# Moving a softmax scaling from VectorE to ScalarE, and choosing anew which sums of x live in DRAM, in a two-layer graph attention kernel

## The chip, the core and the metric

The kernel runs on one core of one Trainium2 chip. The metric is the time of one execution on the device in microseconds (us): the median over runs. The profiled execution's own time is given beside it, because all durations come from that one execution.

## What is computed

A two-layer graph attention network over 512 nodes with 768 features, 16,896 edges (one self-loop per node among them), eight heads of 768 features in the first layer and one in the second, then a residual and a layer norm:

```python
def gat_layer(x, W, a_s, a_d, b, edge_index, concat):
    h = (x @ W).reshape(n, H, C)
    alpha_s = jnp.einsum('nhc,hc->nh', h, a_s)
    alpha_d = jnp.einsum('nhc,hc->nh', h, a_d)
    e = jax.nn.leaky_relu(alpha_s[src] + alpha_d[dst], NEG_SLOPE)
    m = jax.ops.segment_max(e, dst, num_segments=n)
    e = jnp.exp(e - m[dst])
    denom = jax.ops.segment_sum(e, dst, num_segments=n)
    alpha = e / (denom[dst] + EPS)
    out = jax.ops.segment_sum(h[src] * alpha[:, :, None], dst, num_segments=n)
    return out.reshape(n, H * C) + b

h = gat_layer(x, W1, a_src1, a_dst1, b1, edge_index, concat=True)
h = jax.nn.elu(h)
out = gat_layer(h, W2, a_src2, a_dst2, b2, edge_index, concat=True)
return _layernorm(x + out, axis=-1)
```

All of it is in float32.

## The kernel before

**The attention matrix.** Because there are only 512 nodes, the kernel counts the edges into a dense 512 x 512 matrix once (`cnt`), and each head's attention is then a dense softmax. A softmax tile `q` is 128 target nodes by 512 source nodes, so a head has four tiles. For one tile: `lift` (L572, ScalarE) adds the two logits, `leak` (L576, VectorE) is the leaky ReLU, `rank` (L581 VectorE, L583 ScalarE) takes the row maximum and the exponential, and `weigh` (L788 to L798, VectorE) multiplies by the counts with a running row sum (L791), makes the reciprocal `rden` (L794, L795) and scales the tile by it (L797). Then `turn_out` transposes it: ScalarE splits the 32-bit values into 16-bit halves (L812, into `pS` for tiles 0 to 2 and into `nr` for tile 3), and a transposing DMA goes out on SP's queue (L814); later `turn_in` puts the halves together again on ScalarE (L817) into `PT`, the transposed attention matrix.

**The stages of a head.** The loop over heads h = 0 to 6 handles, in this order, three matrix products that belong to three heads:

1. `mixed(h)` (L867, matmuls at L889), the aggregation: features of head h times its attention matrix, as seven products of halves (Strassen's scheme) for each of three column blocks; ELU on ScalarE (L826 to L828), result into `gT` (L829, VectorE). Work of VectorE for other stages is handed in as the list `fill` and dealt out between its steps by `some`.
2. `second(h)` (L442, matmuls at L364): the result times this head's rows of W2, added up in `h2` and `u2` (VectorE, L459). Again seven products, P1, P2, P6, P7, P4, P5, P3, each for two row blocks (`pairs`). P3 goes into the bank that P5 was emptied from. Between these products the softmax of head h + 1 is written: for n = 2 to 6 the loop issues the pair n of products, one tile's `leak` and `rank`, a `weigh` and `turn_out`, and the emptyings `e0` and `e1`. All of `attend` (L985) and of the list `in_second` also goes between them.
3. For head h + 2 the projection x @ W1. For heads 3 to 7 it is `by_thirds` (L407, matmuls at L423; "the thirds stage" below): a scheme of 15 products of blocks of thirds, each product one step of eight matmul records, in the order P8, P13, P9, P2, P4, P12, P6, P0, P1, P10, P5, P14, P11, P7, P3. Five PSUM banks (a, x, b, y, z) take turns: a bank must be emptied (L429 on ScalarE, L431 on VectorE) before the next step may use it. Head 2 has `projection` (L382, matmuls at L364), fourteen products.

Instruction order on each engine is the program's order; nothing is moved by a scheduler.

**The sums of x.** The thirds scheme needs nine sums of blocks of x. They are made once, by VectorE, around head 1 (`x_thirds`, L922): P8, P9 and P13 in place of blocks of `xT`; four in `xF`, the storage of `xS`, which is free after head 2's projection; and five in `gF`, the storage of `gT`. But `gT` is overwritten by every head's aggregation. So the five are stored once to DRAM (`store`, L940, from L936 to L938's results) and loaded again in each round h = 1 to 5 (`reload_x`, L948, `gT<-xd`, 1280 KB) once the second product of head h no longer reads `gT`. The reload stands on SP's queue behind the four transposing DMAs of the softmax and the load of a block of W1 (L161). The five were P7, P1, P6, P3, P14; of these P6 is the first that the thirds stage reads, at its seventh step. The sums are dealt over the stages around head 1: `early` (and `again_`, which restores a block of `xT` that the previous scheme had changed) in head 2's projection, `late_[0]` at its thirteenth product, the next two behind the aggregation of head 1, and four in the second product of head 1.

Of the kernel before, what the change touches and what calls it, by code (L numbers as in the profile page):

```python
# [13 lines left out]
AF = mybir.ActivationFunctionType  # L14
# [22 lines left out]
def gat_pass(  # L37
# [16 lines left out]
    nc = tc.nc  # L54
# [9 lines left out]
    HK = DC // 2  # L64
    HN = N // 2
# [63 lines left out]
    def square(t_, j):  # L129
        return t_[:, j * 2 * TH:(j + 1) * 2 * TH].rearrange("p (k n) -> p k n", k=2)  # L130
# [116 lines left out]
    for j in range(2):  # L247
        nc.vector.tensor_reduce(picks[:, j:j + 1], ident.rearrange("p (j k) -> p k j", k=32)[:, j, :], axis=AX.X,
                                op=ALU.add)
# [5 lines left out]
    xT = keep.tile([P, DC, N], F32, name="xT")  # L255
# [121 lines left out]
    def logits(h, feats, t):  # L377
        for al, a, sign in zip(AL[h], A[h], (1.0, -1.0)):
            nc.vector.scalar_tensor_tensor(scr, feats[:, t, :], sign, a, op0=ALU.mult,  # L379
                                           op1=ALU.mult, accum_out=al[:, t:t + 1])  # L380
# [219 lines left out]
    if not general:  # L600
# [95 lines left out]
        for n, batch in enumerate(batches):  # L696
# [32 lines left out]
            if n + 1 == len(batches):  # L729
                spread(0)  # L730
                q = [lift(0, t) for t in range(NT)]
# [11 lines left out]
    else:  # L743
# [26 lines left out]
        q = [lift(0, t) for t in range(NT)]  # L770
# [17 lines left out]
    def weigh(q, t, scale=True):  # L788

        den = small.tile([P, 1], F32, name="den")  # L790
        nc.vector.scalar_tensor_tensor(q, q, 1.0, cnt[:, t, :], op0=ALU.mult, op1=ALU.mult,  # L791
                                       accum_out=den)
        rden = small.tile([P, 1], F32, name="rden")
        nc.vector.tensor_scalar(rden, den, EPS_DEN, None, op0=ALU.add)  # L794
        nc.vector.reciprocal(rden, rden)  # L795
        if scale:
            nc.vector.tensor_scalar(q, q, rden, None, op0=ALU.mult)  # L797
        return rden  # L798
# [7 lines left out]

    parted = {}

    def turn_out(q, t):
        apart = pS[:, t].rearrange("p k n -> p (k n)") if t < 3 else work.tile([P, N], F32, name="nr")  # L810
        apart = apart.bitcast(U16)
        nc.scalar.copy(apart.rearrange("p (h n) -> p h n", h=2), q.bitcast(U16).rearrange("p (n h) -> p h n", h=2))  # L812
        parted[t] = work.tile([P, N], F32, name="zr", bufs=3).bitcast(U16)
        nc.sync.dma_start(parted[t].rearrange("p (j d) -> p j d", d=P), apart, transpose=True)  # L814
# [103 lines left out]
    gF, xF = gT.rearrange("p c n -> p (c n)"), xS.rearrange("p a k n -> p (a k n)")  # L918
# [3 lines left out]
    def x_thirds():  # L922

        a = {(i, k): xT[:, 2 * k:2 * k + 2, i * TH:(i + 1) * TH] for i in range(2) for k in range(3)}
        X = dict(P2=a[0, 0], P4=a[1, 2], P0=a[1, 1], P8=a[0, 2], P13=a[0, 1], P9=a[1, 0])
        X.update({p: square(gF, j) for j, p in enumerate(("P7", "P1", "P6", "P3", "P14"))})
        X.update({p: square(xF, j) for j, p in enumerate(("P11", "P10", "P12", "P5"))})

        def op(o, u, v, how):
            return lambda: nc.vector.tensor_tensor(o, u, v, op=how)  # L930

        def negative(o, u, v):
            return lambda: nc.vector.scalar_tensor_tensor(o, u, -1.0, v, op0=ALU.mult, op1=ALU.subtract)

        plus, minus = ALU.add, ALU.subtract
        early = [op(X["P7"], a[0, 0], a[0, 1], minus), op(X["P1"], X["P7"], a[0, 2], minus),  # L936
                 op(X["P6"], a[1, 2], X["P1"], minus), op(X["P3"], a[0, 2], a[0, 0], minus),
                 negative(X["P14"], a[0, 2], a[1, 2])]  # L938
        again_ = op(xT[:, :HK, HN:], xT[:, :HK, :HN], xT[:, :HK, HN:], minus)
        store = lambda: nc.sync.dma_start(stored, gF[:, :RELOAD * 2 * TH])  # L940
        late_ = [op(X["P10"], X["P1"], a[1, 1], minus), op(X["P11"], a[0, 1], a[1, 1], plus),
                 negative(X["P12"], a[0, 0], a[1, 1]), op(X["P8"], a[1, 0], a[1, 2], minus),
                 op(X["P5"], X["P10"], X["P8"], plus), op(X["P9"], a[1, 0], a[1, 1], minus),
                 negative(X["P13"], a[0, 0], a[1, 2])]
        return X, early, again_, store, late_

    def reload_x():
        nc.sync.dma_start(gF[:, :RELOAD * 2 * TH], stored)  # L948
# [38 lines left out]
        return [times(slice(0, D), b2_[:, :D], 1.0, V[:, :, 0]), times(L, b2_[:, D:], -1.0, V[:, :, 1]),  # L987
                times(R, b1_[:, D:], -1.0, V2)]

    behind, in_second = [], []  # L990
    for h in range(H - 1):
        if 0 < h < H - 2:
            B3, rest_of_thirds = load_thirds(h + 2)
# [11 lines left out]
        besides, behind = [], []  # L1005
# [25 lines left out]
        q = [lift(h + 1, 0)]  # L1031
        for n in range(2, 7):
            (m0, e0), (m1, e1) = pairs[2 * n:2 * n + 2]
            m0()
            if not last:
                m1()
            if n < 6:
                leak(q[n - 2])
                rank(q[n - 2], n - 2)
            if n < 5:  # L1040
                q.append(lift(h + 1, n - 1))
            if last:

                if n > 4:
                    turn_in(n - 5)
                if n == 6:
                    turn(q[2], 2)
                if n == 6:
                    weigh(q[3], 3)
                m1(lambda: turn(q[3], 3) if n == 6 else None)  # L1050
            if not last and n == 6:
                turn_in(0)
                weigh(q[2], 2)
                turn_out(q[2], 2)
            e0()
            if last and 2 < n < 6:
                weigh(q[n - 3], n - 3)
                if n < 5:
                    turn_out(q[n - 3], n - 3)
            if not last and 3 < n < 6:  # L1060
                weigh(q[n - 4], n - 4)
                turn_out(q[n - 4], n - 4)
            if not last and n == 6:
                weigh(q[3], 3)
                turn_out(q[3], 3)
                if 0 < h:
                    sums = rest_of_thirds()
                    reload_x()
                load_w2(h + 1)()
            e1()  # L1070
            for f in in_second[:1]:
                f()
            del in_second[:1]
            if 0 < h and not last and 2 < n < 6:
                attend[n - 3]()
        if 0 < h and h + 2 < H:
            pairs = by_thirds(h + 2, XB, B3)
            AA, sums3 = left_sums(h + 1)
            B2, sums2 = right(W2[h + 1], "w1")
            for n in range(15):  # L1080
                pairs[n][0]()
                for p in {0: ("P6", "P2"), 1: ("P4",), 4: ("P10",), 5: ("P0",), 6: ("P1",), 9: ("P7",),
                          12: ("P3",)}.get(n, ()):
                    sums[p]()
                if n == 5:
                    BB, rsums_ = right_sums()
                    sums3 += rsums_
                if n in (2, 3, 5, 6, 8, 9, 10):
                    for _ in range(2 if n == 8 else 1):
                        sums3.pop(0)()  # L1090
                if n in (11, 13):
                    logits(h + 2, HS[h + 2], 2 + (n - 11) // 2)
                if n == 14:
                    sums2[0]()
                    behind = sums2[1:]
                pairs[n][1]()
                if n in (1, 2, 4):
                    turn_in((n + 2) // 2)
            assert not sums3
        elif h + 2 < H:  # L1100
            B_, sums = right(W1[h + 2], "w2")
            pairs = projection(h + 2, XA, B_)
            for n in range(14):
                pairs[n][0]()
                if n == 0:
                    for f in attend:
                        f()
                    B2, sums2 = right(W2[h + 1], "w1")
                if n in (1, 3):
                    sums[n // 2]()  # L1110
                if n == 1:
                    AA, sums3 = left_sums(h + 1)
                pairs[n][1]()
                if n in (1, 2, 4):
                    turn_in((n + 2) // 2)
                if n == 5:
                    BB, sums3 = right_sums()
                if 1 <= n < 9:
                    sums3.pop(0)()
                if n == 0:  # L1120
                    XB, early, again_, store, late_ = x_thirds()
                if n in (2, 4, 6, 8, 9):
                    early.pop(0)()
                if n == 9:
                    store()
                if n == 9:
                    again_()
                if n == 12:
                    late_.pop(0)()
                    sums2.pop(0)()  # L1130
                    behind = sums2 + late_[:2]
                    in_second = late_[2:]
                if n in (11, 13):
                    logits(h + 2, HS[h + 2], 2 + (n - 11) // 2)
        else:
            last_sum()
            B2, sums2 = right(W2[H - 1], "w1")
# [162 lines left out]
```

## Time and profile before

| What | Value |
|---|---|
| median of 3 runs | 648.23 us (647.3 to 649.41) |
| the profiled execution | 647.71 us, its span 645.9 us |
| TensorE matmul busy | 630.7 us, 98% |
| TensorE weight loads busy | 434.9 us, 67% |
| VectorE busy | 535.4 us, 83% |
| ScalarE busy | 289.8 us, 45% |
| GpSimd busy | 63.6 us, 10% |
| DMA moved | 109.87 MB, mean 170 GB/s |
| granted TensorE clock | 0.999 |

Columns of a timeline row: start and length in us, engine, line, operation, output <- inputs, how many were merged, and in brackets the idle time just ahead and what ended it. PE is TensorE, PEld its weight loads, DVE VectorE, ACT ScalarE, POOL GpSimd, SP the engine that issues most DMAs; SPq is its instruction queue. A group's row has line, engine, operation, names, shapes and count, then busy us and mean ns of one, then the idle time ahead. In a list of waits: us in total, times, longest. A matmul of float32 stands in the trace as more than one record.

### The profile page before, as it was taken

What the parts mean: (1) busy time and instruction counts of PE and PEld (TensorE: products, weight loads), DVE (VectorE), ACT (ScalarE), POOL (GpSimd) and SP (SyncE); (2) the same over time, 40 slices, a digit from 0 to 9 for tenths busy, and PEclk for the clock granted to TensorE, in tenths of its full rate; (3) what the DMA queues carried; (4) which work ended last, traced back from release to release, by engine and by line L of the source; (5) the groups of instructions that cost most, each with busy time, mean ns of one, the idle gap of its engine ahead of it and who ended that gap; (6) DMA issues with size and microseconds to landing.
All of it is one profiled execution on the core that took longest, in us unless ns stands there. A gap on an engine that the chain in (4) does not pass through costs nothing.

```text
span 645.9 us, 7667 instructions
## 1 busy us (share of the span) xinstructions
PE 630.7 (98%) x2509; PEld 434.9 (67%) x2509; DVE 535.4 (83%) x1162; ACT 289.8 (45%) x486; POOL 63.6 (10%) x105
## 2 busy tenths in 40 slices
PE   8999999999999999999999999999999999999995
PEld 5555586556756786588857886588857886544553
DVE  8989889988889778878789778878789778876775
ACT  5875655520726045441726145441726145543440
POOL 1210011010200220010200220010200210000000
PEclk9999999999999999999999999999999999999999
DMA  8994488796905976198815986198924991310122
GB/s 300 324 219 97 103 219 289 154 268 223 238 9 112 315 209 183 21 271 222 230 76 115 308 225 172 20 259 230 231 79 108 326 294 33 95 59 1 28 63 77
DMA packets 86845, 109.87 MB, mean 170 GB/s; under 512 B 40151, under 2 KB 67983, under 8 KB 86031
## 3 DMA queue, kind: packets, MB, share of 16 engines
q1 hardware_dynamic: 70590, 87.42, 41.9%
q0 software_dynamic: 15776, 21.30, 19.8%
q10 hardware_dynamic: 432, 0.59, 0.3%
q8 instruction: 22, 0.36, 0.2%
q14 instruction: 25, 0.20, 0.1%
HBM read 95.12 MB, written 2.90 MB: 152 GB/s over the span
## 4 chain that ended last, share of the span: by engine, by line
PE 88%; DMA 5%; DVE 4%; ACT 1%; issue 1%; DVEq 0%; SPq 0%; ACTq 0%
PE mm L364 41%; PE mm L889 19%; PE mm L423 15%; DMA gT<-xd 5%; PE mm L835 3%; PE mm L1246 3%; PE held L364 2%; PE tr L664 1%; PE bc L233 1%; PE held L544 1%; PE bc L664 0%; DVE h L459 0%; ACT os L636 0%; DVE scr L379 0%; PE mm L262 0%
## 5 line engine op out<-in xcount | busy, mean ns | idle before, releaser
L364 PE MATMUL mm<-w,gT 128*128 128x384 f32 x252 | 83.6, 486 | 0.0
L364 PEld LDWEIGHTS mm<-w,gT 128*128 128x128 f32 x252 | 47.9, 190 | 31.9
L583 ACT ACTIVATE q<-q,nmax 128x512 f32<-128x512 f32 x36 | 25.8, 721 | 96.3 <-DVE nmax L581 96.3
L889 PE MATMUL mm<-PT,hs 128*128 128x256 f32 x252 | 61.3, 379 | 0.0
L364 PE MATMUL mm<-w1t,gS 128*128 128x384 f32 x180 | 60.6, 487 | 0.0
L429 ACT ACTIVATE hs<-mm 128x512 f32<-128x512 f32 x30 | 17.9, 596 | 91.6 <-PE mm L423 91.2
L889 PEld LDWEIGHTS mm<-PT,hs 128*128 128x128 f32 x252 | 47.8, 190 | 7.3 <-issue 0.4
L364 PEld LDWEIGHTS mm<-w1t,gS 128*128 128x128 f32 x180 | 34.1, 190 | 24.0 <-DVE w1t L356 0.5
L459 DVE TENSOR_TENSOR h<-h,mm 128x384 f32<-128x384 f32 x72 | 39.0, 549 | 11.8 <-PE mm L364 11.5
L431 DVE TENSOR_TENSOR hs<-hs,mm 128x512 f32<-128x512 f32 x45 | 30.8, 684 | 21.3 <-PE mm L423 21.3
L889 PE MATMUL mm<-pS,gS 128*128 128x256 f32 x168 | 43.2, 380 | 0.0
L817 ACT COPY PT<-zr 128x1024 uint16<-128x1024 uint16 x34 | 39.3, 1155 | 2.6 <-DMA zr<-pS 1.9
L423 PE MATMUL mm<-w2r,xT 128*128 128x256 f32 x160 | 37.8, 379 | 0.0
L423 PE MATMUL mm<-w2r,gT 128*128 128x256 f32 x160 | 37.5, 382 | 0.0
L812 ACT COPY pS<-q 128x1024 uint16<-128x1024 uint16 x26 | 27.1, 1044 | 18.3 <-DVE q L797 18.3
L889 PEld LDWEIGHTS mm<-pS,gS 128*128 128x128 f32 x168 | 31.8, 190 | 4.7 <-DVE pS L862 0.4
L423 PEld LDWEIGHTS mm<-w2r,xT 128*128 128x128 f32 x160 | 30.4, 190 | 5.2
L423 PEld LDWEIGHTS mm<-w2r,gT 128*128 128x128 f32 x160 | 30.0, 190 | 5.8 <-DVE hs L431 1.9
L364 PE MATMUL mm<-w1t,gT 128*128 128x384 f32 x96 | 32.3, 486 | 0.0
L364 PE MATMUL mm<-w,gS 128*128 128x384 f32 x84 | 29.3, 495 | 1.1 <-DVE h L459 1.1
L638 DVE TENSOR_SCALAR os<-nodes,idx 128x512 bf16<-128x512 f16 x104 | 29.0, 352 | 1.4 <-PE tr L664 1.4
L893 ACT COPY u<-mm 128x256 f32<-128x256 f32 x21 | 7.8, 372 | 49.2 <-PE mm L889 49.2
(233 smaller groups left out, 1260.5 us busy)
## 6 DMA issues: line engine op xcount, KB each, us to landing
w2r<-in_L_gnn_W_dram SPq DMA_DIRECT2D x48, 384.0 KB, 11.0
w<-in_L_gnn_W_dram SPq DMA_DIRECT2D x43, 384.0 KB, 10.9
gT<-xd SPq DMA_DIRECT2D x5, 1280.0 KB
w1t<-in_L_gnn_W_dram SPq DMA_DIRECT2D x9, 576.0 KB
w<-in_L_gnn_W_dram POOLq DMA_DIRECT2D x8, 576.0 KB, 8.5
w1t<-in_L_gnn_W_dram POOLq DMA_DIRECT2D x7, 576.0 KB, 9.6
w2t<-in_L_gnn_W_dram SPq DMA_DIRECT2D x15, 256.0 KB, 7.1
w2t<-in_L_gnn_W_dram POOLq DMA_DIRECT2D x15, 256.0 KB, 8.8
```

The lines of the kernel that those rows point to most:

```text
L364: nc.tensor.matmul(ps[:, :HALF], A_[p][:, k, i * P:(i + 1) * P], B_[p][:, k, :], start=start and k == 0, stop=k == HK - 1, skip_group_chec ...
L423: nc.tensor.matmul(bank[chain][:, i * TH:(i + 1) * TH], A_[p][:, k, i * P:(i + 1) * P], B_[p][:, k, :], start=first and i == k == 0, stop= ...
L429: nc.scalar.activation(out(o), ps, AF.Copy, scale=how)
L431: nc.vector.tensor_tensor(out(o), out(o), ps, op=how)
L459: nc.vector.tensor_tensor(a, a, ps, op=ALU.subtract if p == "P7" else ALU.add)
L583: nc.scalar.activation(q, q, AF.Exp, bias=nmax, scale=-1.0)
L638: nc.vector.tensor_scalar(o, nodes, idx[:, c:c + 1], None, op0=ALU.is_equal)
L812: nc.scalar.copy(apart.rearrange("p (h n) -> p h n", h=2), q.bitcast(U16).rearrange("p (n h) -> p h n", h=2))
L817: nc.scalar.copy(PT.rearrange("p s n -> p (s n)").bitcast(U16).rearrange("p (s n h) -> p s n h", s=NT, h=2)[:, :, t * P:(t + 1) * P, :], p ...
L835: nc.tensor.matmul(ps[:, :N], HS[h][:, s, c * P:(c + 1) * P], PT[:, s, :], start=(s == 0), stop=(s == NT - 1))
L889: nc.tensor.matmul(bank[p][:, :HN], A_[p][:, k, c * P:(c + 1) * P], B_[p][:, k, :], start=over is None and k == 0, stop=k == 1, skip_group ...
L1246: nc.tensor.matmul(ps[:, :cols.stop - cols.start], PT[:, s, t * P:(t + 1) * P], h2[:, s, cols], start=(s == 2), stop=(s == 1))
```

## The change

There are two edits.

The scaling of a softmax tile by `rden` moves for heads 1 to 6: `weigh` is called with `scale=False` and returns `rden`, and `turn_out` begins with an ACTIVATE of ScalarE that copies `q` onto itself times `rden`, ahead of the copy that splits it. Heads 0 and 7 keep VectorE's scaling, the second layer had none.

The sums of x: in `gF`, and so in DRAM, are now P7, P1, P3, P14, P11; in `xF` are P10, P6, P12, P5. The first sum that the thirds stage reads from `gT` is thus P1, at its ninth step. The work is dealt out anew: six operations in `early` (P7, P1, P3, P14, the restoring one, P11), the store behind the last of them, P10 and P6 at the thirteenth and fourteenth product of head 2's projection, P8 in the aggregation of head 1, P13 and P9 in its second product, and P12 and P5 at the third and eighth step of head 3's thirds stage.

```diff
-    def turn_out(q, t):
+    def turn_out(q, t, rden=None):
+        if rden is not None:
+            nc.scalar.activation(q, q, AF.Copy, scale=rden)
...
-        X.update({p: square(gF, j) for j, p in enumerate(("P7", "P1", "P6", "P3", "P14"))})
-        X.update({p: square(xF, j) for j, p in enumerate(("P11", "P10", "P12", "P5"))})
+        X.update({p: square(gF, j) for j, p in enumerate(("P7", "P1", "P3", "P14", "P11"))})
+        X.update({p: square(xF, j) for j, p in enumerate(("P10", "P6", "P12", "P5"))})
...
         early = [op(X["P7"], a[0, 0], a[0, 1], minus), op(X["P1"], X["P7"], a[0, 2], minus),
-                 op(X["P6"], a[1, 2], X["P1"], minus), op(X["P3"], a[0, 2], a[0, 0], minus),
-                 negative(X["P14"], a[0, 2], a[1, 2])]
-        again_ = op(xT[:, :HK, HN:], xT[:, :HK, :HN], xT[:, :HK, HN:], minus)
+                 op(X["P3"], a[0, 2], a[0, 0], minus), negative(X["P14"], a[0, 2], a[1, 2]),
+                 op(xT[:, :HK, HN:], xT[:, :HK, :HN], xT[:, :HK, HN:], minus), op(X["P11"], a[0, 1], a[1, 1], plus)]
...
-                weigh(q[2], 2)
-                turn_out(q[2], 2)
+                turn_out(q[2], 2, weigh(q[2], 2, scale=False))
...
-                weigh(q[n - 4], n - 4)
-                turn_out(q[n - 4], n - 4)
+                turn_out(q[n - 4], n - 4, weigh(q[n - 4], n - 4, scale=False))
...
-                weigh(q[3], 3)
-                turn_out(q[3], 3)
+                turn_out(q[3], 3, weigh(q[3], 3, scale=False))
...
+                if n in in_third:
+                    in_third.pop(n)()
...
-                if n in (2, 4, 6, 8, 9):
+                if n in (2, 4, 6, 8, 9, 10):
                     early.pop(0)()
-                if n == 9:
+                if n == 10:
                     store()
-                if n == 9:
-                    again_()
                 if n == 12:
-                    late_.pop(0)()
+                    late_["P10"]()
                     sums2.pop(0)()
-                    behind = sums2 + late_[:2]
-                    in_second = late_[2:]
+                    behind = sums2 + [late_["P8"]]
+                if n == 13:
+                    late_["P6"]()
+                    in_second, in_third = [late_["P13"], late_["P9"]], {2: late_["P12"], 7: late_["P5"]}
```

More of the change, by code (lines that the diff above doesn't have):

```diff
@@ L936, in x_thirds @@
         early = [op(X["P7"], a[0, 0], a[0, 1], minus), op(X["P1"], X["P7"], a[0, 2], minus),
-                 op(X["P6"], a[1, 2], X["P1"], minus), op(X["P3"], a[0, 2], a[0, 0], minus),
-                 negative(X["P14"], a[0, 2], a[1, 2])]
-        again_ = op(xT[:, :HK, HN:], xT[:, :HK, :HN], xT[:, :HK, HN:], minus)
+                 op(X["P3"], a[0, 2], a[0, 0], minus), negative(X["P14"], a[0, 2], a[1, 2]),
+                 op(xT[:, :HK, HN:], xT[:, :HK, :HN], xT[:, :HK, HN:], minus), op(X["P11"], a[0, 1], a[1, 1], plus)]
         store = lambda: nc.sync.dma_start(stored, gF[:, :RELOAD * 2 * TH])
[L941 to L945, printed above, removed]
+        late_ = dict(P10=op(X["P10"], X["P1"], a[1, 1], minus), P6=op(X["P6"], a[1, 2], X["P1"], minus),
+                     P8=op(X["P8"], a[1, 0], a[1, 2], minus), P13=negative(X["P13"], a[0, 0], a[1, 2]),
+                     P9=op(X["P9"], a[1, 0], a[1, 1], minus), P12=negative(X["P12"], a[0, 0], a[1, 1]),
+                     P5=op(X["P5"], X["P10"], X["P8"], plus))
+        return X, early, store, late_
     def reload_x():
@@ L988, in attended @@
                 times(R, b1_[:, D:], -1.0, V2)]
-    behind, in_second = [], []
+    behind, in_second, in_third = [], [], {}
     for h in range(H - 1):
@@ L1120, in gat_pass @@
                 if n == 0:
-                    XB, early, again_, store, late_ = x_thirds()
-                if n in (2, 4, 6, 8, 9):
+                    XB, early, store, late_ = x_thirds()
+                if n in (2, 4, 6, 8, 9, 10):
                     early.pop(0)()
-                if n == 9:
+                if n == 10:
                     store()
-                if n == 9:
-                    again_()
                 if n == 12:
-                    late_.pop(0)()
+                    late_["P10"]()
                     sums2.pop(0)()
-                    behind = sums2 + late_[:2]
-                    in_second = late_[2:]
+                    behind = sums2 + [late_["P8"]]
+                if n == 13:
+                    late_["P6"]()
+                    in_second, in_third = [late_["P13"], late_["P9"]], {2: late_["P12"], 7: late_["P5"]}
                 if n in (11, 13):
```

## The prediction

> **What bounds the kernel now.** I read the page first (busy shares, chain), then who waited for whom, then the timelines engine by engine around each reload, because a wait of TensorE says where, and only the timeline says why.
>
> ```profile
> PE 630.7 (98%) x2509; PEld 434.9 (67%) x2509; DVE 535.4 (83%) x1162; ACT 289.8 (45%) x486; POOL 63.6 (10%) x105
> PE 88%; DMA 5%; DVE 4%; ACT 1%; issue 1%; DVEq 0%; SPq 0%; ACTq 0%
> PE mm L423 <- DMA gT<-xd: 4.2, 5, 1.1
> ```
>
> TensorE is busy 98% of 645.9 us and holds 88% of the chain that ended last. Its largest wait is for the reload of the stored sums of x into gT, five times. TensorE's timeline says what that costs. In the thirds stage a step is eight matmul records; rows are start, length, records, wait.
>
> ```profile
> 208.22 1.89 PE L423 MATMUL mm<-w2r,xT 128*128 128x256 f32 x8
> 209.95 1.89 PE L423 MATMUL mm<-w2t,xS 128*128 128x256 f32 x8
> 212.95 1.97 PE L423 MATMUL mm<-w2t,gT 128*128 128x256 f32 x8 [1.10 <-DMA gT<-xd]
> ...
> 283.08 1.89 PE L423 MATMUL mm<-w2t,xS 128*128 128x256 f32 x8
> 285.77 1.96 PE L423 MATMUL mm<-w2t,gT 128*128 128x256 f32 x8 [0.79 <-DMA gT<-xd]
> 287.57 1.89 PE L423 MATMUL mm<-w2r,xT 128*128 128x256 f32 x8
> ...
> 355.91 1.89 PE L423 MATMUL mm<-w2t,xS 128*128 128x256 f32 x8
> 358.32 1.97 PE L423 MATMUL mm<-w2t,gT 128*128 128x256 f32 x8 [0.52 <-DMA gT<-xd]
> ...
> 428.45 1.89 PE L423 MATMUL mm<-w2t,xS 128*128 128x256 f32 x8
> 431.37 1.97 PE L423 MATMUL mm<-w2t,gT 128*128 128x256 f32 x8 [1.03 <-DMA gT<-xd]
> ...
> 501.51 1.89 PE L423 MATMUL mm<-w2t,xS 128*128 128x256 f32 x8
> 504.18 1.96 PE L423 MATMUL mm<-w2t,gT 128*128 128x256 f32 x8 [0.78 <-DMA gT<-xd]
> ```
>
> Undisturbed steps start 1.73 us apart (208.22 to 209.95). The seventh step (P6, the first that reads gT) should start 1.73 after the sixth (P12); it starts 3.00, 2.69, 2.41, 2.92 and 2.67 after it. That is 1.27 + 0.96 + 0.68 + 1.19 + 0.94 = 5.0 us. The step after the wait also runs 1.80 in place of 1.73 (285.77 to 287.57), 0.07 x 5 = 0.35. So the five waits cost 5.4 us; the page's own sum of 4.2 is the lower bound, since it counts from modelled ends.
>
> **Part 1: the stored sums.** P6 now lives in xS, which is never overwritten after head 2, and P11 takes its place in gT. The first product that reads gT becomes P1, the ninth step, two steps or 3.46 us later. Does the reload land by then? It lands just ahead of the seventh step as that now starts: 212.95, 285.77, 358.32, 431.37, 504.18. Without the wait P1 would start 1.73 x 3 = 5.19 after the sixth step: 215.1, 288.3, 361.1, 433.6, 506.7. That leaves 2.2 to 2.8 us of slack in each head, if the reload isn't issued later. So all five waits go: **-5.4 us** (at least -4.2). What is late next is the bank that the eighth step fills: VectorE must have emptied P12 from it.
>
> ```profile
> 283.36 0.69 DVE L431 TENSOR_TENSOR hs<-hs,mm 128x512 f32<-128x512 f32 x1 [1.69 <-PE mm L423]
> ...
> 285.43 0.68 DVE L431 TENSOR_TENSOR hs<-hs,mm 128x512 f32<-128x512 f32 x1
> ```
>
> That emptying ends at 286.11 and the eighth step would start at 283.08 + 3.46 = 286.54, so 0.4 us remain; VectorE waited for TensorE (1.69) just before, so the distance is fixed by TensorE and doesn't shrink.
>
> **Part 2: the scaling on ScalarE.** Four scalings leave VectorE and four enter ScalarE in each of six heads. Head 3's softmax shows the path to the reload, which SP issues behind the four transposes.
>
> ```profile
> 271.41 0.49 DVE L797 TENSOR_SCALAR q<-q,rden 128x512 f32<-128x512 f32 x1
> 271.81 0.55 DVE L459 TENSOR_TENSOR h<-h,mm 128x384 f32<-128x384 f32 x1
> ...
> 271.93 1.04 ACT L812 COPY pS<-q 128x1024 uint16<-128x1024 uint16 x1 [1.27 <-DVE q L797]
> 272.88 1.16 ACT L817 COPY PT<-zr 128x1024 uint16<-128x1024 uint16 x1
> ...
> 276.37 1.04 ACT L812 COPY nr<-q 128x1024 uint16<-128x1024 uint16 x1 [0.88 <-DVE q L797]
> ...
> 277.44 1.23 SPq L814 DMA_TRANSPOSE zr<-nr  x1
> 278.84 0.46 SPq L161 DMA_DIRECT2D w2t<-in_L_gnn_W_dram  x1
> 279.35 0.48 SPq L948 DMA_DIRECT2D gT<-xd  x1
> ```
>
> On VectorE a scaling takes 0.40 us from start to start (271.41 to 271.81). On ScalarE no row has this operation. The nearest:
>
> ```profile
> L826 ACT ACTIVATE nr<-zr,nb1T 128x512 f32<-128x512 f32 x21 | 15.2, 724 | 2.4 <-DVE zr L906 2.4
> L828 ACT ACTIVATE nr<-nr 128x512 f32<-128x512 f32 x27 | 16.6, 616 | 0.0
> ```
>
> L828 has no per-row operand, L826 has one (its bias), as the scaling has (rden). I take 0.72 us, with 0.62 below and the 1.16 of L817, the longest data movement there, above. The copy of the scaled q must wait for its end, so 0.76 each. In order on ScalarE: q1's scaling can start at 271.41 - 0.40 = 271.01, since VectorE is one scaling ahead, and takes until 271.77; its copy, 0.95 from start to start (271.93 to 272.88), until 272.72; L817, 1.16, until 273.88; scaling and copy of q2, 1.71, until 275.59; scaling of q3 until 276.35. So the last copy starts at 276.35 where it started at 276.37: VectorE gets there earlier (three times 0.40), ScalarE takes over as the last to arrive, and transposes, the load of L161 and the reload leave SP at the same time as before. At 1.16 per scaling they would leave 3 x 0.44 = 1.3 us later, inside the slack of 2.2. Behind the last copy ScalarE's queue holds the emptying of P8 and three turn-ins (L817), whose readers come several steps later. So on the path of the reload this part is worth nothing, either way.
>
> The Trainium skill (ScalarE: Activation LUTs, Rules for kernel authors) says to put a plain multiplication on VectorE and not on ScalarE. By the rows the operation does get longer there; by that rule the change gives time away, and this is the fourth rival below.
>
> It is worth something where VectorE ends last. In the second product the first matmul of P3 waits for L459 to empty P5.
>
> ```profile
> 266.54 4.03 PE L364 MATMUL mm<-w1t,gS 128*128 128x384 f32 x12
> 270.43 4.19 PE L364 MATMUL mm<-w,gS 128*128 128x384 f32 x12
> ```
>
> 12 records take 3.87 from start to start, so 270.41 was due; 0.02 and the longer 4.19 make 0.18 us. VectorE will be 0.40 ahead (q0's scaling), so this goes in the four heads that look like this: **-0.7 us** (bounds 0 and -0.7).
>
> **Part 3: the four stages of sums of x**, once, around head 1. Before its aggregation VectorE gets one operation more (P6 at the fourteenth product, of 0.60 from start to start), and P11 comes into an idle time of 1.38 us (150.17), where it costs nothing. The store goes out behind P11, at about 149.4 in place of 147.48. The window row (its last columns are the DMA engines' share and GB/s) shows the old one done by 152.0; gT is first written at 159.70, and SP's next instruction, a load, started at 154.03, so two microseconds more are hidden.
>
> ```profile
> 152.00:153.00 1.00, 1.00 (x5) 0.60 (x4) 1.00 (x4) 0.00 (x0) 0.00 (x0) 1.00 0.00 0
> ...
> 150.17 0.56 DVE L402 TENSOR_TENSOR hs<-mm,hs 128x384 f32<-128x384 f32 x1 [1.38 <-PE mm L364]
> ...
> 159.70 0.42 DVE L829 SCALAR_TENSOR_TENSOR gT<-nl,zl 128x256 f32<-128x256 f32 x1
> 168.08 1.35 DVE L357 TENSOR_TENSOR w1t<-w1t,w 128x1152 f32<-128x1152 f32 x1
> ...
> 147.48 0.33 SPq L940 DMA_DIRECT2D xd<-gT  x1
> 154.03 2.73 SPq L145 DMA_DIRECT2D w2r<-in_L_gnn_W_dram  x6
> ...
> 159.41 1.13 PE L889 MATMUL mm<-PT,gS 128*128 128x256 f32 x4
> ```
>
> From 150.17 to 159.4 VectorE's timeline shows no idle time, and the aggregation's P3 at 159.41 already starts only when VectorE has read its bank. The extra 0.60 arrives in full: +0.6. Then the aggregation's fill list has seven entries in place of eight, so the sum of L357 (1.35 us, 1.27 from start to start) moves from the second column to the third, to where P11, of 0.60, stood. VectorE has next to nothing in hand there: +0.5 (0 to 1.27 - 0.60 = 0.7). Together **+1.1 us**.
>
> In head 1's second product the list shrinks from four sums to two.
>
> ```profile
> 192.20 4.03 PE L364 MATMUL mm<-w1t,gS 128*128 128x384 f32 x12
> 197.30 4.19 PE L364 MATMUL mm<-w,gS 128*128 128x384 f32 x12 [1.06 <-DVE h L459]
> ...
> 194.27 0.68 DVE L930 TENSOR_TENSOR xT<-xT 128x512 f32<-128x512 f32 x1
> 194.88 0.55 DVE L985 SCALAR_TENSOR_TENSOR scr<-w2t,w2t 128x384 bf16<-128x384 f32 x1
> ```
>
> Due was 192.20 + 3.87 = 196.07, so 1.23 are lost. A sum of 0.60 (194.27 to 194.88) and one scaling of 0.40 leave the stretch ahead of it: **-1.0 us**. P12 and P5 move into head 3's thirds stage, where VectorE waits for TensorE before 283.36 in the like stage of head 4; they are early enough for steps 6 and 11: nothing.
>
> **Sum.** -5.4 - 0.7 + 1.1 - 1.0 = -6.0 us. The profiled execution took 647.71 us (span 645.9 and 1.8 around it), so 641.7. The median of the three runs is 648.23, 0.5 above it: I forecast **642.2 us**. With the bounds of the terms (-6.9 to -3.5) the forecast's own range is 641.3 to 644.7, and a little wider for the runs' scatter (647.3 to 649.41).
>
> **Rivals.**
> 1. *The wait moves on.* P1 waits in P6's place, or the eighth step waits for its bank. For it: the five waits differ by 0.6 us (0.68 to 1.27), so the reload's time isn't constant. Against: 2.2 us of slack, and 0.4 for the bank. With half of the 5.4 gone again: 645. Chance 0.12.
> 2. *ScalarE becomes the bound; slower than before.* Three scalings of q1 to q3 lie in a row on ScalarE ahead of the reload's issue. At s us each the reload lands 3 (s - 0.72) later; past s = 1.55 it has used the slack of 2.5 and every head pays, and past 2.1 the kernel is slower by over 0.3% (3 x 1.38 - 2.5 = 1.6 a head, 8.2 in five, against 6.0 gained and 1.9). At 2.5: 5.3 - 2.5 = 2.8 a head, 14 in five, 656. Against: no ScalarE group on data is over 1.16. Chance 0.06.
> 3. *VectorE is the bound.* Then 24 scalings of 0.40 come off the end, -9.6, and with them half of the five waits, -2.5: 636. For it: 83% busy. Against: TensorE's steps come evenly, 1.73 apart, through stretches where VectorE idles. The Trainium skill (Perfetto Trace Analysis, Identifying the Most-Contended Engine) says to judge TensorE by the busy share of weight loads and not by that of matmuls, and to work on the fullest engine; by that, PEld's 67% would leave VectorE's 83% first. Chance 0.04.
> 4. *The scaling costs on the path what it costs more on ScalarE.* 24 x (0.76 - 0.49) = 6.5 us takes back all of the gain: 648.7, no change. Against: the last copy's time as worked out above. Chance 0.07.
>
> **Chances and range.** The forecast has 0.71. A measurement of this kernel can tell about 0.3% (1.9 us) from no change. Faster by more: forecast, rivals 1 and 3, 0.87; within: rival 4, 0.07; slower: rival 2, 0.06. The range 640.5 to 645.6 takes in the forecast with its bounds and most of rival 1.
>
> **What would show it.** Right: no matmul waits for gT<-xd; P6 starts 1.73 after P12 in all five heads; the reload leaves 3.7 before P12 starts, as it does now (279.35 and 283.08); the scaling's group on ScalarE near 0.72; head 1's aggregation about 1 us longer (159.41 to 160.0) and its second product 1 us shorter. Wrong: a wait of P1 for the reload, ScalarE without idle time from q1's copy past 278, or a step of the thirds stage late by VectorE.

## The result and the profile after

The changed kernel takes 641.86 us (median of six runs, 641.29 to 642.58), the kernel before 648.20 (six runs); the ratio is 0.9891 with a 95% interval of 0.986 to 0.9922. That is the ratio of the means; the medians give 0.990, because one of the six runs before took 653.17. The forecast was 642.2. The profiled execution took 642.08 us with a span of 640.3, against 647.71 and 645.9.

The page of the changed kernel, busy shares and the chain that ended last:

```profile
PE 629.4 (98%) x2509; PEld 436.3 (68%) x2509; DVE 525.5 (82%) x1138; ACT 306.0 (48%) x510; POOL 63.6 (10%) x105
PE 96%; ACT 1%; DVE 1%; issue 0%; DVEq 0%; ACTq 0%
```

VectorE lost 9.9 us of work and ScalarE gained 16.2, so the two engines together work 6 us more than before; yet the kernel is 6 us faster. What changed is the second line: the 5% of the chain that were DMA are gone, VectorE's 4% fell to 1, and TensorE's share rose from 88 to 96%. In the list of TensorE's waits no row names gT any more, and the one of 1.1 us for L459 in head 1's second product is gone too. The two that are new stand in head 1's aggregation, 0.5 us for VectorE's L900 and 0.4 for its L905.

The chain in order of time (start, length, what) gives the length of a stage. First two rounds of the kernel before, then the same stretch of the changed kernel:

```profile
247.36 27.26 PE mm L364 x84
274.62 4.74 PE mm L423 x22
279.35 6.28 DMA gT<-xd
...
285.77 16.03 PE mm L423 x72
301.80 18.38 PE mm L889 x84
```

```profile
246.36 27.09 PE mm L364 x84
273.45 26.15 PE mm L423 x120
```

Before, the thirds stage took 301.80 - 274.62 = 27.18 us, 6.28 of it a transfer; now it is one unbroken row of 26.15. The second product went from 27.26 to 27.09. Added up from the starts of the stages on TensorE:

| Stage | before | after | difference | forecast |
|---|---|---|---|---|
| aggregation of head 1 | 19.02 | 20.11 | +1.09 | +1.1 |
| second product of head 1 | 28.47 | 27.28 | -1.19 | -1.0 |
| thirds stage, head 3 | 27.50 | 26.15 | -1.35 | } -5.4 |
| thirds stages, heads 4 to 7 | 108.67 | 104.70 | -3.97 | } |
| second products of heads 2 to 5 | 109.04 | 108.36 | -0.68 | -0.7 |
| sum | | | -6.1 | -6.0 |

The span shrank by 5.6, since head 1's aggregation began 0.45 later. That shift is there already at 61 us (the same chain piece starts at 61.00 before and at 61.44 after), ahead of everything that the change touches; the same kernel (the one with the early P6 and the later L357 sum, below), profiled twice, began that aggregation at 154.38 and at 153.47, so half a microsecond is within the scatter of the opening.

**The handover on ScalarE.** Rows of the changed kernel in the softmax of head 3, VectorE, ScalarE, SP and TensorE:

```profile
269.68 0.16 DVE L795 RECIPROCAL rden<-rden 128x1 f32<-128x1 f32 x1
269.76 0.54 DVE L459 TENSOR_TENSOR h<-h,mm 128x384 f32<-128x384 f32 x1
...
269.88 0.72 ACT L811 ACTIVATE q<-q,rden 128x512 f32<-128x512 f32 x1 [0.74 <-DVE rden L795]
270.63 1.04 ACT L814 COPY pS<-q 128x1024 uint16<-128x1024 uint16 x1
271.59 1.16 ACT L819 COPY PT<-zr 128x1024 uint16<-128x1024 uint16 x1
...
274.35 0.72 ACT L811 ACTIVATE q<-q,rden 128x512 f32<-128x512 f32 x1
275.10 1.04 ACT L814 COPY nr<-q 128x1024 uint16<-128x1024 uint16 x1
...
278.08 0.47 SPq L949 DMA_DIRECT2D gT<-xd  x1
...
273.29 1.89 PE L423 MATMUL mm<-w2r,xT 128*128 128x256 f32 x8
```

Behind q1's scaling no row of ScalarE has idle time ahead of it (q2's scaling and copy, left out, follow in the same way): ScalarE is now the engine that the last copy waits for, as worked out. The copy starts 1.81 us after the thirds stage (275.10 - 273.29); before it was 1.92. And the reload leaves 4.79 us after the stage's start; before it was 4.90. So the reload was not made earlier by anything that matters. Its reader was made later:

```profile
281.92 3.62 PE L423 MATMUL mm<-w2t,xS 128*128 128x256 f32 x16
285.38 1.89 PE L423 MATMUL mm<-w2r,xT 128*128 128x256 f32 x8
287.10 1.89 PE L423 MATMUL mm<-w2r,gT 128*128 128x256 f32 x8
```

P12 and P6 are one row of sixteen records now, both from xS; the eighth step starts on time, and P1, the first from gT, starts at 287.10 without a wait. The other four heads show the same, but for head 6, whose eighth step is 0.1 us late by VectorE (its stage takes 26.25).

### The profile page after: what moved, and what is told of

It is laid out like the page before. It is cut to its first block, busy times and chain, and to the rows that moved or that the text cites. A ratio compares the mean times of both kernels' runs of the same rounds, so it can differ in the third digit from the quotient of the medians.

```text
span 640.3 us, 7665 instructions
## 1 busy us (share of the span) xinstructions
PE 629.4 (98%) x2509; PEld 436.3 (68%) x2509; DVE 525.5 (82%) x1138; ACT 306.0 (48%) x510; POOL 63.6 (10%) x105
## 4 chain that ended last, share of the span: by engine, by line
PE 96%; ACT 1%; DVE 1%; issue 0%; DVEq 0%; ACTq 0%
PE mm L364 44%; PE mm L423 20%; PE mm L891 19%; PE mm L837 3%; PE mm L1246 3%; PE held L364 2%; PE tr L664 1%; PE bc L233 1%; PE held L544 1%; PE bc L664 0%; ACT os L636 0%; PE mm L262 0%; PE tr L1170 0%; DVE w1t L357 0%; DVE os L638 0%
## 5 line engine op out<-in xcount | busy, mean ns | idle before, releaser
L459 DVE TENSOR_TENSOR h<-h,mm 128x384 f32<-128x384 f32 x72 | 38.9, 547 | 13.3 <-PE mm L364 13.0
```

Of the source, the lines that this page charges most:

```text
L459: nc.vector.tensor_tensor(a, a, ps, op=ALU.subtract if p == "P7" else ALU.add)
```

## The experiments

The theory: five waits for the reload carry the change, because its first reader moved two steps back; the scaling is worth little, because what it takes off VectorE ScalarE adds in front of the same transfer. The main rival: VectorE is the bound, and the scaling is what counts. Each ratio below is to the kernel before, run on the same chip.

**Scaling alone.**

```diff
-    def turn_out(q, t):
+    def turn_out(q, t, rden=None):
+        if rden is not None:
+            nc.scalar.activation(q, q, AF.Copy, scale=rden)
...
-                weigh(q[2], 2)
-                turn_out(q[2], 2)
+                turn_out(q[2], 2, weigh(q[2], 2, scale=False))
```

(and the same at the two other calls in the loop)

> Only the scaling moves to ScalarE; the sums of x stay as before. Theory 1 (the five waits for the reload carry the change): the first reader of gT is still P6, so the five waits stay, each at most 0.1 us shorter; the four second products lose their 0.18 us (-0.7) and head 1's second product gains the 0.5 us that one scaling takes from VectorE. Together -1.2 to -1.9: 646.3 to 647.0 us. Rival (VectorE is the bound): 24 scalings of 0.5 us come off the end, 636 us.

Measured: 647.37 us against 648.58, ratio 0.9981 (0.9963 to 0.9999). TensorE's waits in it:

```profile
PE mm L423 <- DMA gT<-xd: 4.3, 4, 2.5
PE mm L423 <- DVE hs L854: 0.7, 1, 0.7
PE mm L364 <- DVE h L459: 0.5, 1, 0.5
```

The wait for the reload is as long as ever (the second row is the fifth of them: the matmul that reads gT in head 3's stage, put down to an operation that ended about then). The wait of head 1's second product halved, 1.1 to 0.5. Counted from step to step, the five waits cost 5.8 us in this profile and 5.0 before, which takes back most of what the second products gained there: 0.59 us in head 1 and 0.68 in the four others together. The time is 0.4 us above the expected stretch, within the scatter of this kernel (645.43 to 649.43 in ten runs); against the kernel before on its own chip the gain is 1.2 us, the least that was expected, and its interval reaches almost to nothing. It is 11 us from the rival's 636. VectorE isn't the bound.

**Sums alone.**

```diff
-        X.update({p: square(gF, j) for j, p in enumerate(("P7", "P1", "P6", "P3", "P14"))})
-        X.update({p: square(xF, j) for j, p in enumerate(("P11", "P10", "P12", "P5"))})
+        X.update({p: square(gF, j) for j, p in enumerate(("P7", "P1", "P3", "P14", "P11"))})
+        X.update({p: square(xF, j) for j, p in enumerate(("P10", "P6", "P12", "P5"))})
```

(with the changed kernel's dealing of them, and the scaling on VectorE)

> Only the sums of x are chosen and dealt anew; the scaling stays on VectorE. Theory 1: all five waits go (-5.3), head 1's aggregation gets 1.1 us longer and its second product 0.6 shorter: -4.8, 643.4 us. Rival (VectorE is the bound): its work is the same as before, so no change, 648.2 us. If the two parts don't touch each other, the gains of this kernel and of the one with the scaling alone add up to 6.3.

Measured: 643.17 us, ratio 0.9918 (0.9901 to 0.9934); 643.4 was expected. Two rows of its chain:

```profile
246.83 27.25 PE mm L364 x84
274.09 26.15 PE mm L423 x120
```

The thirds stage has its full gain (26.15), the second product none (27.25): each edit acts in its own stage. The two gains, 5.4 and 1.2, add up to 6.6 against the 6.3 of the whole (differences of medians; the whole comes from another set of runs). VectorE has as much to do here as before (535.5 us busy and 535.4), and most of the gain is there.

**One more operation per tile on ScalarE, and two more.** A multiplication by ones changes no value; it only makes ScalarE's share longer.

```diff
             nc.scalar.activation(q, q, AF.Copy, scale=rden)
+            nc.scalar.activation(q, q, AF.Copy, scale=ones)
```

> The changed kernel with one more ACTIVATE of 0.72 us on each of the 24 tiles (a multiplication by ones) behind the scaling: ScalarE's part per tile is 1.48 us in place of 0.72. Theory 1: the reload leaves SP 3 x 0.76 = 2.3 us later and still lands ahead of P1 (slack 2.3 to 2.6): within 0.5 us of the changed kernel, 641.9 to 642.4. Rival (what ScalarE does for the softmax lies on the path): 24 x 0.76 = 18 us, 660 us; a half of it, if only the last two tiles count: 651.

> The changed kernel with two more such ACTIVATEs per tile: 2.24 us per tile on ScalarE. Theory 1: everything behind the last copy moves 4.6 us later. That is past two guards: P8's emptying on ScalarE, which VectorE needs before P4's bank is free, then comes about 1.8 us late for the fifth step, and the reload about 2 us late for P1; both lie in one line, so each of five heads loses about 2: +10, 652 us (649 to 655). Rival (ScalarE has idle time enough, 48% busy, and nothing is late): 642 us. Rival (all of it on the path): 24 x 1.52 = 36, 678 us.

Measured: 644.42 us with one more (ratio 0.9938, 0.9921 to 0.9955) and 661.65 with two (1.0195, 1.0178 to 1.0212). Both forecasts failed: the times are above the theory's numbers, by 2 us and by 10 (7 above the end of its range). They fit no rival either: 651 or 660 for one more, 642 or 678 for two. The kernel with one more, SP and then TensorE in the same stage as above, TensorE in head 2's projection, and the sixth step of head 3's stage:

```profile
281.36 0.47 SPq L950 DMA_DIRECT2D gT<-xd  x1
...
274.31 1.89 PE L423 MATMUL mm<-w2r,xT 128*128 128x256 f32 x8
...
281.21 1.89 PE L423 MATMUL mm<-w2r,xT 128*128 128x256 f32 x8
283.06 3.72 PE L423 MATMUL mm<-w2t,xS 128*128 128x256 f32 x16
...
288.35 1.89 PE L423 MATMUL mm<-w2r,gT 128*128 128x256 f32 x8
...
126.38 4.04 PE L364 MATMUL mm<-w2r,xT 128*128 128x384 f32 x12
131.32 4.14 PE L364 MATMUL mm<-w2r,xT 128*128 128x384 f32 x12 [0.90 <-ACT hs L397]
...
211.21 3.72 PE L423 MATMUL mm<-w2t,xS 128*128 128x256 f32 x16 [0.38 <-ACT hs L429]
```

The reload leaves 7.05 us after the stage's start, 2.26 later as expected, and P1 still doesn't wait for it: that part of the theory holds. But P12 starts at 283.06 where 282.94 was due and its row is 0.10 longer: 0.23 lost in this head. P12 fills the bank that ScalarE empties of P2, and that emptying now comes late in ScalarE's queue. Heads 5 to 7 lose 0.15 to 0.23 each in the same place; head 3 loses 0.66 (the last row). In head 2's projection the third product waits for ScalarE to empty the first (L397): 131.32 where 126.38 + 3.87 = 130.25 was due, 1.1 us, and the whole projection is 1.2 longer. The five stages are 1.5 us longer than in the changed kernel, and 1.5 + 1.2 = 2.7 is all of the 2.6. With two more, the fifth step comes first, as expected, but the sixth loses once more behind it, and the projection loses more than both (rows of head 4's stage, of the projection, and of P1 in head 6's stage):

```profile
289.51 1.99 PE L423 MATMUL mm<-w2r,xT 128*128 128x256 f32 x8 [1.68 <-DVE hs L431]
291.88 3.72 PE L423 MATMUL mm<-w2t,xS 128*128 128x256 f32 x16 [0.38 <-ACT hs L429]
...
133.73 5.83 PE L364 MATMUL mm<-w2r,xT 128*128 128x384 f32 x12 [3.17 <-ACT hs L397]
...
447.15 1.97 PE L423 MATMUL mm<-w2r,gT 128*128 128x256 f32 x8 [1.39 <-DVE pS L865]
```

The fifth steps are 1.8 to 2.9 us late, 10.7 in five heads, which is what was expected. Not expected were the sixth steps (3.8 with their longer rows) and the projection (5.1). The reload makes P1 late in one head only, head 6: 1.6 us, 8.5 us after the reload was issued (the profile puts the wait down to a VectorE operation that P1 doesn't read, so the reload is inferred). In the other heads the late fifth and sixth steps have already pushed P1 behind the reload. Together that is 21 us, against 19.8 on the clock. So the point from which a longer scaling costs is set by the emptyings behind the last copy, not by the reload. The next run tests that.

**One more operation, with the turn-ins two steps later.**

```diff
-                if n in (1, 2, 4):
-                    turn_in((n + 2) // 2)
+                if n in (3, 4, 6):
+                    turn_in({3: 1, 4: 2, 6: 3}[n])
```

> The kernel with one more ACTIVATE per tile, with the three turn-ins of the thirds stage (L819 in the changed kernel) two steps later on ScalarE. That kernel lost 0.23 us in each of five heads where P12 waits for the emptying of P2 on ScalarE, and 1.1 in head 2's projection. Theory (ScalarE's in-order queue reaches that emptying late because turn-ins stand ahead of it; the reload isn't late): the five losses go, -1.2 us against 644.4, so 643.2. Rival (the later reload is what costs): no change, 644.4.

Measured: 643.25 us, ratio 0.9922 (0.9893 to 0.9951). TensorE in the same stage:

```profile
281.24 1.89 PE L423 MATMUL mm<-w2r,xT 128*128 128x256 f32 x8
282.97 3.62 PE L423 MATMUL mm<-w2t,xS 128*128 128x256 f32 x16
```

The sixth step is on time again (281.24 + 1.73) and its row is 3.62 long. The reload leaves as late as in the kernel with one more, 7.05 us after the stage's start, and heads 4 to 7 are as short as in the changed kernel: what they lost was ScalarE's queue order, and not the transfer. Head 3 gets back only 0.23 of its 0.66; its sixth step is on time, but the eighth is now late. VectorE, then TensorE there:

```profile
208.35 0.69 DVE L431 TENSOR_TENSOR hs<-hs,mm 128x512 f32<-128x512 f32 x1 [3.46 <-ACT hs L429]
...
214.69 2.00 PE L423 MATMUL mm<-w2r,xT 128*128 128x256 f32 x8
```

The eighth step was due at 214.37. VectorE, which empties its bank of P12, had waited 3.46 us for ScalarE's late emptying of P8 and worked without idle time from there, in this head with the sum P12 in between. So the expected 1.2 us is met on the clock (644.42 to 643.25, on two chips), while the stages got 1.0 us shorter. Beside the changed kernel on its own chip (641.72) 1.5 us remain: the projection's 1.2 and head 3's 0.4.

**Giving back the 1.1 us of head 1's aggregation.** First P6 in a gap of VectorE's:

```diff
-        X.update({p: square(xF, j) for j, p in enumerate(("P10", "P6", "P12", "P5"))})
+        X.update({p: square(xF, j) for j, p in enumerate(("P10", "P12", "P6", "P5"))})
...
+                if n == 7:
+                    late_["P6"]()
                 if n == 13:
-                    late_["P6"]()
```

> The changed kernel with P6 summed at the eighth product of head 2's projection (where VectorE idles 0.78 us) in place of the fourteenth; for that P6 and P12 swap their places in xS. Theory 1: the first column of head 1's aggregation is 6.54 us long as before the change (7.14 in the changed kernel), the third keeps its 0.5 for the sum of L357: -0.6 us in all, 641.3 us. Rival (the aggregation's loss comes from the moved L357 sum or the later store alone): first column stays at 7.1, no change.

Measured: 641.06 us, ratio 0.9898 (0.9882 to 0.9915). Then the long sum (L357) moved behind P8 as well:

```diff
-                    behind = sums2 + [late_["P8"]]
+                    behind = [late_["P8"]] + sums2
```

> As the kernel with the early P6, and P8 stands ahead of the L357 sum in the aggregation's fill list, so that the 1.27 us operation falls behind the last column, where VectorE waits 0.9 us for TensorE. Theory 1: the third column is 6.2 us long again (6.68 in the changed kernel) and nothing is lost behind it: -1.1 us against the changed kernel, 640.8 us. Rival (VectorE just has the operation to do somewhere): the loss moves into the second product, 641.3 us.

Measured: 640.81 us, ratio 0.9889 (0.9872 to 0.9905). TensorE in the aggregation, first of the changed kernel, then with P6 early, then with both:

```profile
154.28 1.03 PE L891 MATMUL mm<-PT,hs 128*128 128x256 f32 x4
...
161.42 1.03 PE L891 MATMUL mm<-PT,hs 128*128 128x256 f32 x4
...
167.71 1.03 PE L891 MATMUL mm<-PT,hs 128*128 128x256 f32 x4
...
173.43 1.13 PE L891 MATMUL mm<-PT,gS 128*128 128x256 f32 x4 [0.37 <-DVE zr L905]
174.39 7.90 PE L364 MATMUL mm<-w,gT 128*128 128x384 f32 x24
```

```profile
153.47 1.03 PE L891 MATMUL mm<-PT,hs 128*128 128x256 f32 x4
...
160.01 1.03 PE L891 MATMUL mm<-PT,hs 128*128 128x256 f32 x4
```

```profile
166.29 1.03 PE L891 MATMUL mm<-PT,hs 128*128 128x256 f32 x4
...
171.47 1.03 PE L891 MATMUL mm<-PT,gS 128*128 128x256 f32 x4
172.34 7.90 PE L364 MATMUL mm<-w,gT 128*128 128x384 f32 x24
```

The first column takes 7.14 in the changed kernel (154.28 to 161.42) and 6.54 with P6 early: the extra operation was all of that loss, not the store. The third takes 6.68 (167.71 to 174.39) and 6.05 with L357 behind it (166.29 to 172.34), and the wait of 0.37 is gone. The second product stays at 27.28, so nothing comes back. The last fence is of a second run of that kernel, beside the changed kernel on one chip:

> The changed kernel once more, beside the three others on one chip: 641.9 us (641.3 to 642.6).

> The kernel with the early P6 and the later L357 sum, on the same chip as the changed kernel. Theory: 1.1 to 1.2 us below the changed kernel, as its aggregation of head 1 is shorter by that. Rival (the difference between the two calls was one of the chips): no difference.

Measured: 641.72 us for the changed kernel (ratio 0.9894, 0.9865 to 0.9923) and 640.73 for this one (0.9883, 0.9854 to 0.9911). It is the fastest of all here; on the clock the 1.0 us is near the scatter of the medians, and what shows it is the length of the stage.

**What is left in the thirds stage.** P7 starts 0.14 late in each head, because its bank is emptied behind 1.9 us of logits.

```diff
-                if n in (11, 13):
-                    logits(h + 2, HS[h + 2], 2 + (n - 11) // 2)
+                if n == 13:
+                    logits(h + 2, HS[h + 2], 3)
...
                 pairs[n][1]()
+                if n == 11:
+                    logits(h + 2, HS[h + 2], 2)
```

> That kernel, and in each thirds stage VectorE empties P14 before it forms the logits of the third node tile, not behind them. P7 now starts 0.14 late in each of five heads and its stretch is 0.10 longer, since the bank it fills is emptied behind 1.9 us of logits. Theory: 5 x 0.24 = 1.2 us less than the kernel with early P6 and later L357. Rival (VectorE has no room, the logits then make the next emptying late): the same loss shows at P3 or in the aggregation, no change.

Measured: 642.43 us, ratio 0.9907 (0.9878 to 0.9935): 1.7 us slower than without it. VectorE, then TensorE:

```profile
293.05 0.69 DVE L431 TENSOR_TENSOR hs<-hs,mm 128x512 f32<-128x512 f32 x1 [0.98 <-PE mm L423]
...
296.14 0.68 DVE L431 TENSOR_TENSOR hs<-hs,mm 128x512 f32<-128x512 f32 x1
...
294.57 1.89 PE L423 MATMUL mm<-w2r,gT 128*128 128x256 f32 x8
296.87 1.99 PE L423 MATMUL mm<-w2r,gT 128*128 128x256 f32 x8 [0.41 <-DVE hs L431]
```

P7 is on time, 1.72 after P11 in that kernel, but VectorE now idles 0.98 us for P14's product, in which it used to form logits; the logits then push the emptying of P11 (296.14) behind the time at which P3 wants its bank. The theory fell, and the rival's mechanism held, though it expected no change: the loss moved one step on and grew by 0.43 a head (the stage takes 26.58 in place of 26.15, from 272.29 to 298.87).

## Why the prediction was right, and where it wasn't

- **The reload (-5.4).** Measured -5.3 in the five stages. The reasoning held in each link: the reload left at the same time, its reader came 3.46 us later, and the bank of the eighth step, with 0.4 us in hand, didn't become the next wait (0.1 us in head 6 is all that it cost), so the first rival fell too. The sums alone gave this on their own.
- **The scaling's cost on ScalarE.** 0.72 us was taken from the nearest row with one per-row operand; the group measured 720 ns on 24 instructions. The last copy was forecast at 0.02 earlier relative to before and came 0.1 earlier.
- **The scaling's worth.** A VectorE scaling was counted as 0.40 us; it took 0.52. The next operation now starts 0.08 after the reciprocal's start (269.68 to 269.76), where it started 0.60 after it before (271.21 to 271.81): the dependent start of the scaling went too. That is most of the difference in head 1's second product (-1.19 for -1.0): the scaling alone took 0.59 us from that stage, the sums alone 0.62. The four other second products gave 0.68 for 0.7.
- **Head 1's aggregation (+1.1).** Measured +1.09, and the split too: 0.60 in the first column, 0.50 in the third. The two runs that take each part back show the two causes apart.
- **The third and fourth rivals** (VectorE the bound; the longer operation on the path) fell with the first two experiments. The rule of the Trainium skill (ScalarE: Activation LUTs, Rules for kernel authors), a multiplication belongs on VectorE, is right about the operation (0.72 against 0.49 here) and would have kept a gain of 1.2 us from being made: where an engine ends last decided here, not where an operation is shorter.
- **The second rival's number was wrong.** I put the point from which ScalarE's lateness costs at 1.55 us per scaling, from the reload's slack. At 1.48 us it cost 2.6 us, and at 2.24 it cost 20 where the rival's formula gives 10. The step that failed is the sentence that the readers of what stands behind the last copy "come several steps later". It names P8's emptying and three turn-ins, but not the emptyings of P9 and P2, which stand between the turn-ins, and I had not set the due times of all of them beside the queue. The emptying of P2 is due before the sixth step and the one of P1 in head 2's projection before the third product there, both sooner than the reload before the ninth. At the 0.72 us of the change neither is late, so the forecast didn't suffer.
- **A sign of being wrong that told nothing.** ScalarE without idle time past 278 was to speak against the forecast. It is without idle time until 277.70 in the changed kernel, 4.41 us after the stage's start, which is 278.86 on the clock of the kernel before; there it was busy until 278.96 as well. What stands behind the last copy keeps it busy in both kernels, so the sign was badly chosen.
- **The number.** That 642.2 came within 0.4 us of the median is in part luck: the runs before lie between 647.30 and 653.17, and the errors of the terms, 0.1 and 0.2 us, have opposite signs. The ends of the forecast's own range, -6.9 and -3.5, don't follow from the stated bounds, which give -6.5 and -3.9; the result doesn't turn on it.

## What to carry to other kernels

A transfer that is always a little late could be mended here from the reader's end: put what it brings where it is read last, and keep what is read first resident. Then price a longer queue on the helping engine by the due time of every instruction behind it, not only by that of the transfer that one looks at. And look at the timeline of both stretches before an operation is moved on an engine that works in order: P6's sum was worth its full 0.60 us where VectorE had no idle time and cost nothing where it had 0.78, while the logits, moved to where VectorE then had too little room, cost 0.43 a head.

## What was not expected

The runs of the kernels that still wait for the reload scatter more. The scaling alone lay between 645.43 and 649.43 us in ten runs, and the kernel before between 647.50 and 651.24 in thirteen, while the sums alone lay between 642.80 and 643.77 in four, on the same chip. In the profile of the scaling alone the five waits were not alike: TensorE rows of heads 6 and 7 (P12, then P6),

```profile
427.93 1.89 PE L423 MATMUL mm<-w2t,xS 128*128 128x256 f32 x8
432.36 1.97 PE L423 MATMUL mm<-w2t,gT 128*128 128x256 f32 x8 [2.54 <-DMA gT<-xd]
...
502.33 1.89 PE L423 MATMUL mm<-w2t,xS 128*128 128x256 f32 x8
504.45 1.97 PE L423 MATMUL mm<-w2t,gT 128*128 128x256 f32 x8 [0.23 <-DMA gT<-xd]
```

P6 came 2.70 and 0.39 us late. In the first of them SP took 1.43 us to issue the load ahead of the reload, where it took 0.46 in the others, and the transfer itself 7.2 us where it took 5.8 in the second. That the larger scatter of the times comes from this was not tested.
